# B and C of a Mamba block, four channel blocks side by side in the TensorE array, with a new set of task times

## The chip, the cores and the metric

The kernel runs on one core of one Trainium2 chip. The metric is the device time of one execution in microseconds (us). A core has a matrix engine (TensorE, PE in the profile, with its weight loads as PEld), a vector engine (VectorE, DVE), an activation engine (ScalarE, ACT), a general engine (GpSimd, POOL) and a queue engine that starts transfers here (SyncE, SP). Each engine works through its own list of instructions in order and waits on semaphores for the others.

## The reference

A block of four residual layers on x of 2 x 2048 tokens and 512 channels, in float32:

```python
x = x + rwkv(layernorm(x))          # a recurrence over the tokens (wkv)
x = x + ffn(layernorm(x))           # silu(x Wg) * (x Wu), times Wd; 1376 wide, weights looked up in a table of 16
x = x + mamba(layernorm(x))
x = x + ffn(layernorm(x))           # same weights

def mamba(s):                       # 1024 channels, 16 states per channel, rank 128
    x, gate = s @ in_proj           # then x: causal convolution of 4 taps, + bias, silu
    u = silu(conv(x) + b)
    ssm = u @ x_proj.T              # 160 columns: 128 of dt_lr, 16 of B, 16 of C
    delta = softplus(dt_lr @ dt_proj.T + dt_b)
    # for every token: h = h * exp(delta * A) + (delta * u) * B ;  y = sum over the states of h * C
    return ((y + u * D) * silu(gate)) @ out_proj.T
```

The change concerns `ssm`, and within it the 32 columns of B and C.

## The kernel before

The kernel has two stages. The first computes the RWKV layer in chunks of 512 tokens, the looked-up weights, and the first feed-forward of the first 256 tokens. It ends near 700 us. The second stage is the subject: 16 chunks of 256 tokens (TB), each with a first feed-forward (`f1`), the front of the Mamba layer (`front`), its scan over the tokens (`scan`), the output projection (`project`) and a second feed-forward (`f2`). A 2048-token sequence is eight chunks, and the state is carried from chunk to chunk.

**Order of the work.** Nothing is scheduled automatically. `Line.at(t, fn)` enters a task with a time; at the end all tasks are sorted by their times and emitted in that order, so the times in the dictionary `AT` fix the order of every engine's list. The unit is a slot: one chunk's scan has 32 slots (SLOTS), one for each pair of channel block and quarter of the states. While chunk w is scanned, the same 32 slots also hold the projection and second feed-forward of chunk w-1, the front of chunk w+1, and the first feed-forward of chunk w+2. `step_size` of a chunk is cut into two halves of four channel blocks, each of two quarters q: the first half is computed in the window before (`step0`), the second in the chunk's own window (`step1`; `step1a` in the first chunk). Weights are loaded in pieces of 256 KB through a ring of 18 buffers by `Stream`, some 8 slots ahead (LEAD).

**The scan.** Per channel block c4 and quarter q of the states: `grow` (L852) multiplies delta*u by B for four states on POOL and adds the carried state (L855); `decay` (L862) computes exp(delta*A) on ACT into PSUM, two states at a time, with three buffers; `run` does the recurrence (L872), the product with C (L873) and keeps the last state (L875) on DVE; `fold` adds the states on POOL (L882, L887, L888). In the last chunk PE adds them instead (`spread`, L896). `load` fetches B and C, spread over the partitions, from DRAM (bcd) with transfers of 512 KB (bc). After a channel pair, DVE closes y (L918, L919).

**The other tasks** named below: a layernorm has its statistics on DVE (L601, L602: mv), its root on POOL (L603 to L606: rs, nrs), its scaling on ACT (L612, L613: nm, xn), a transposition on PE (L618) and a copy on ACT (L619: xnT). A feed-forward has gate and up products (L659: pg, gu), a silu on ACT (L677, L680: hT), a product on DVE (L686, L689) and the down product (L639: po), whose sum DVE adds to x (L643). The front has its products (L712), three taps on DVE (L732) and silu on ACT (L738: u). `step_size` has products with dt_proj (L776), activations (L780 to L786), a logarithm (L790: lt), corrections on DVE (L793, L794), the close on POOL (L799, L800), and the carried state's factor (L807 on ACT, L814 on POOL). The silu of the gate is L848 (sg). Exp, log and silu need different tables in ACT, so that ACT_TABLE_LOAD stands between them.

**The task that is changed**, `x_product`, multiplies u by x_proj: for each of two column groups (128 columns of dt_lr, then 32 of B and C) eight products, one per channel block, are added in PSUM (L752). Then ACT copies B and C (bcs, L755) and dt_lr (dtl, L757), and SP stores bcs to DRAM (L759). All of this is one task at slot `x`.

Of the kernel before, what the change touches and what calls it, by code (L numbers as in the profile page):

```python
# [8 lines left out]
F32 = mybir.dt.float32  # L9
I32 = mybir.dt.int32  # L10
AF = mybir.ActivationFunctionType
ALU = mybir.AluOpType
# [3 lines left out]
P = 128  # L16
# [8 lines left out]
ND = DI // P  # L25
NS = 16
RK = 128
# [3 lines left out]
TB = 256  # L31
# [29 lines left out]
def block_kernel(ctx: ExitStack, tc: tile.TileContext, a: dict, out: bass.AP):  # L61
    nc = tc.nc
    V, S, G, PE = nc.vector, nc.scalar, nc.gpsimd, nc.tensor
# [4 lines left out]
    ident = const.tile([P, P], F32, name="ident")  # L68
# [14 lines left out]
    with ExitStack() as pa:  # L83
        wpool = pa.enter_context(tc.tile_pool(name="a_w", bufs=1))
# [4 lines left out]
        wk = pa.enter_context(tc.tile_pool(name="a_wk", bufs=11))  # L89
# [28 lines left out]
        for k in range(4):  # L118
# [7 lines left out]
                  y=0.413, x=-3.46, stats=-3.029, stat=0.083, each=0.062, copy=0.119, fmul=0.867,  # L126
                  opened=-3.355, mean=-2.71, scale=-2.177, turn=-2.106, out=3.964, outs=0.02,
                  add=0.188, bits=(-3.02, 29.13), marks=(-4.09, 10.75), ahead=0.503, ff=(11.44,
                  31.66), ffln=10.705, fgate=0.559, fdown=2.36, times=0.284)
        NBITS = 8  # L130
        line = Line()
# [361 lines left out]
    with ExitStack() as pb:  # L493
        NWS, LEAD = 18, 8.0
        wpool = pb.enter_context(tc.tile_pool(name="b_w", bufs=1))
# [10 lines left out]
        wk = pb.enter_context(tc.tile_pool(name="b_wk", bufs=2))  # L506
# [10 lines left out]
        for tl, nm in ((cw, "conv_w"), (cb, "conv_b"), (dtb, "dt_b"), (dcol, "D"), (acol, "A_log")):  # L517
# [7 lines left out]
        wxp = wpool.tile([P, ND, RK + 2 * NS], F32, name="wxp")  # L525
        wdt = wpool.tile([P, DI], F32, name="wdt")
        nc.sync.dma_start(wxp, a["x_proj"].rearrange("(k p) d -> p k d", p=P))
        nc.sync.dma_start(wdt, a["dt_proj"])

        nchunk = NTOK // TB  # L530
        NJ = TB // P


        AT = dict(total=0.13, y=1.08, decay=1.1, grow=1.5, fold=2.75, gates=(2.59, 0.82, 24.96,
                  26.99), front=(6.05, 6.48, 7.41, 8.16), f2=(8.75, 8.93, 12.67, 14.17, 14.38,
                  16.88), f1=(21.88, 21.98, 24.35, 24.27, 29.8, 25.63), f2d=16.39, f1d=30.14,
                  x=11.42, step0=20.87, step1=9.48, step=2.56, exp=0.62, log=1.16, fix=2.12,
                  du=3.52, carry=3.52, zero=4.38, proj=2.49, frontln=3.04, f2ln=5.92, f1ln=18.95,
                  store=29.71, taps=1.03, conv=0.04, unit=1.86, add=0.6, silu=-0.29, hT=0.36,
                  scale=0.19, turn=0.82, g1ln=-5.01, g1=0.94, g1s=1.17, late=7.66, step1a=-5.72,  # L540
                  ahead=12.53, spread=2.01, gsilu=0.64)
        line = Line()
        xs = {}

        def mm(name="ps"):
            return mmp.tile([P, 2, TB], F32, tag="mm", name=name)
# [45 lines left out]
        def ln(t, ci, box):  # L592
# [29 lines left out]
            for j in range(NJ):  # L622
                line.at(t + AT["scale"] + 0.1 * j, scale, j)
                line.at(t + AT["turn"] + 0.1 * j, turn, j)

        def residual(times, ci, lhsT, src):

            po, n = [], len(times)
            w = [stream.piece(t, t + 0.01, src(i)) for i, t in enumerate(times)]

            def first():
                for j in range(NJ):
                    po.append(mmp.tile([P, C], F32, tag="mm", name="po"))

            def one(i):
                lw = lhsT(i)
                m = lw.shape[0]
                for j in range(NJ):
                    PE.matmul(po[j], lhsT=lw[:, j * P : (j + 1) * P], rhs=w[i]["w"][:m],  # L639
                              start=(i == 0), stop=(i == n - 1))  # L640

            def add(j):
                V.tensor_tensor(xs[ci][j], xs[ci][j], po[j], ALU.add)  # L643

            line.at(times[0], first)
            for i, t in enumerate(times):
                line.at(t + 0.005, one, i)
            for j in range(NJ):
                line.at(times[-1] + 0.3 + AT["add"] + 0.15 * j, add, j)

        def feed_forward(t_ln, times, td, dtd, ci):
# [39 lines left out]
            for i, ti in zip(range(0, NF, 2), times):  # L691
                d = 0.65 if i + 1 < NF else 0.3
                for j in range(2):
# [3 lines left out]
                    line.at(tj + 0.005, half, i, j, w)  # L697
                line.at(ti + d + AT["silu"], gate, i)
                line.at(ti + 2 * d + AT["hT"], close, i)
            residual([td + dtd * i for i in range(NF)], ci, lambda i: hT[i], lambda i: wff[i][:, 2 * C :])  # L700

        def front(t_ln, times, tx, ci, box):

            ln(t_ln, ci, box)
            xin, ps = {}, {}

            def product(cp, w):
                ps[cp] = mm()
                for j in range(2):
                    wj = w[j]["w"].rearrange("p (k f) -> p k f", k=KC)  # L710
                    for k in range(KC):
                        PE.matmul(ps[cp][:, j, :], lhsT=wj[:, k, :], rhs=box["xnT"][:, k, :],  # L712
                                  start=(k == 0), stop=(k == KC - 1))

            def copy(cp):
                two = slice(2 * cp, 2 * cp + 2)
                x = xin[cp] = wk.tile([P, 2, TB + KCONV - 1], F32, tag="xin", name="xin")
                if ci % (SEQ // TB) == 0:
                    G.memset(x[:, :, : KCONV - 1], 0.0)
                else:  # L720
                    S.copy(x[:, :, : KCONV - 1], cst[:, two, :])
                S.copy(x[:, :, KCONV - 1 :], ps[cp])
                S.copy(cst[:, two, :], x[:, :, TB:])
                for j in range(2):
                    c = 2 * cp + j
                    S.activation(ps[cp][:, j, :], ps[cp][:, j, :], AF.Identity,  # L726
                                 bias=cb[:, c : c + 1], scale=cw[:, c, KCONV - 1 : KCONV])

            def taps(cp, j):
                c = 2 * cp + j  # L730
                for i in range(KCONV - 1):
                    V.scalar_tensor_tensor(ps[cp][:, j, :], xin[cp][:, j, i : i + TB],  # L732
                                           cw[:, c, i : i + 1], ps[cp][:, j, :], ALU.mult, ALU.add)

            def unit(cp):
                if cp == 0:
                    box["u"] = up.tile([P, ND, TB], F32, tag="u", name="u")
                S.activation(box["u"][:, 2 * cp : 2 * cp + 2, :], ps[cp], AF.Silu)  # L738

            for cp, tp_ in enumerate(times):  # L740
                w = [stream.piece(tp_, tp_ + 0.01, a["in_proj"][2 * cp + j]) for j in range(2)]
                line.at(tp_ + 0.005, product, cp, w)
                line.at(tp_ + AT["conv"], copy, cp)
                for j in range(2):
                    line.at(tp_ + AT["taps"] + 0.35 * j, taps, cp, j)
                line.at(tp_ + AT["unit"], unit, cp)

            def x_product():
                p2 = mm()
                for j, (lo, m) in enumerate(((0, RK), (RK, 2 * NS))):  # L750
                    for c in range(ND):
                        PE.matmul(p2[:m, j, :], lhsT=wxp[:, c, lo : lo + m], rhs=box["u"][:, c, :],  # L752
                                  start=(c == 0), stop=(c == ND - 1))
                bcs = wk.tile([2 * NS, TB], F32, tag="bcs", name="bcs", bufs=1)
                S.copy(bcs, p2[: 2 * NS, 1, :])  # L755
                box["dtl"] = wk.tile([P, TB], F32, tag="dtl", name="dtl")
                S.copy(box["dtl"], p2[:, 0, :])  # L757
                box["bcd"] = bcd_p.tile([2 * NS, TB], F32, tag="bcd", name="bcd")
                nc.sync.dma_start(box["bcd"], bcs)  # L759

            line.at(tx, x_product)

        def step_size(t, box, half):

# [185 lines left out]
        for w in range(-1, nchunk + 1):  # L950
# [14 lines left out]
            if -1 <= w < nchunk - 1:  # L965
                boxes[w + 1] = {}
                late = AT["late"] if w == 0 else 0.0
# [69 lines left out]
```

## Time and profile before

| | |
|---|---|
| three runs | 3670.57 us median (3670.43 to 3672.81) |
| profiled execution, its own time | 3668.55 us |
| its span, first to last instruction | 3666.7 us |
| granted TensorE clock, mean | 0.973 |
| instructions | 43341 |
| start of the scan of the first chunk | 789.8 us |
| last scan instruction starts | 3584.3 us |
| grows of one chunk (POOL, L852) | 32 of 2.36 us |
| scans of one chunk (DVE, L872) | 64 of 1.22 us |
| x_product's matrix instructions (L752) | 512, in 16 chunks |

How to read the lines that follow. The totals of the page name an engine, its busy time, its share of the span and its instructions. A line of the windows names a stretch, its length, then the busy time of PE, PEld, DVE, ACT and POOL with the number of instructions, then the clock, the share of DMA and GB/s. A line of waits names who waited (engine, tile, line) and for whom, the total in us, the number of times, and the longest. A line of the timeline has start and length in us, engine, line, operation, output<-input, shapes, and in brackets the idle time ahead of it with its releaser. A float32 product is two passes of the array, and the profile counts each pass, so that "x16" is eight products.

### The profile page before, as it was taken

Reading aid. Unit: us, or ns where it says so; the run is one execution under the profiler, and the core shown is the slowest. Engines: PE = TensorE matmul, PEld = TensorE weight load, DVE = VectorE, ACT = ScalarE, POOL = GpSimd, SP = SyncE. Lnnn points to the kernel's source line nnn. Section 1 sums busy time; section 2 is a strip of 40 time slices with the busy share of each in tenths; the row PEclk is TensorE's granted clock in tenths of the full one; section 3 lists DMA queues with packets and bytes.
Section 4 is the critical chain, followed back from the end, with each engine's and each line's share of the span. In section 5 each row is a group of like instructions: output and inputs, shape, how many; then the busy total and the mean of one; then the engine's idle time right before and its main releaser. Section 6 shows DMA issues by size and latency. Waiting matters only on the chain. (4 is left out here: it accounts for less than half of the span.)

```text
span 3666.7 us, 43341 instructions
## 1 busy us (share of the span) xinstructions
PE 3389.0 (92%) x12577; PEld 2292.7 (63%) x12592; DVE 3215.8 (88%) x4880; ACT 2744.4 (75%) x4870; POOL 3015.4 (82%) x2801
## 2 busy tenths in 40 slices
PE   7898999777999999999999999999999999998698
PEld 3443444365676767676767666676767676766475
DVE  7999999459898989999999999999989898989882
ACT  5566776487787878787888878787878787878661
POOL 2555666358999999999999999999999999999850
PEclk9999999898999999999999999999999999999799
DMA  2121111244656565565656565656565555554441
GB/s 112 41 72 66 58 66 66 89 164 139 192 185 190 183 189 184 179 203 166 216 169 206 168 213 167 209 177 200 176 204 179 190 184 190 187 187 136 137 147 60
DMA packets 266876, 572.49 MB, mean 156 GB/s; under 512 B 29840, under 2 KB 31504, under 8 KB 266640
## 3 DMA queue, kind: packets, MB, share of 16 engines
q1 hardware_dynamic: 266640, 569.73, 47.9%
q8 instruction: 101, 1.65, 0.2%
q14 instruction: 135, 1.11, 0.1%
HBM read 543.14 MB, written 26.48 MB: 155 GB/s over the span
## 5 line engine op out<-in xcount | busy, mean ns | idle before, releaser
L872 DVE TENSOR_TENSOR_SCAN h<-h,db 128x512 f32<-128x512 f32 x1024 | 1252.2, 1223 | 124.1 <-ACT h L862 100.1
L852 POOL TENSOR_TENSOR db<-du,bc 128x1024 f32<-128x1024 f32 x512 | 1206.3, 2356 | 37.1 <-PE y L896 35.5
L862 ACT ACTIVATE h<-dl,acol 128x256 f32<-128x256 f32 x2048 | 955.4, 475 | 302.7 <-DVE hst L875 265.1
L873 DVE TENSOR_TENSOR db<-h,bc 128x512 f32<-128x512 f32 x1024 | 708.0, 691 | 35.9
L882 POOL TENSOR_TENSOR db<-db 128x512 f32<-128x512 f32 x480 | 609.4, 1270 | 0.0
L639 PE MATMUL po<-w,hT 128*128 128x512 f32 x1364 | 600.6, 592 | 0.0
L659 PE MATMUL pg<-xnT,w 128*128 128x256 f32 x2480 | 555.2, 381 | 1.8 <-ACT xnT L619 1.8
L659 PE MATMUL gu<-xnT,w 128*128 128x256 f32 x2480 | 555.7, 379 | 0.0
L659 PEld LDWEIGHTS pg<-xnT,w 128*128 128x128 f32 x2480 | 472.9, 191 | 69.6 <-ACT xnT L619 6.4
L659 PEld LDWEIGHTS gu<-xnT,w 128*128 128x128 f32 x2480 | 472.3, 190 | 69.0 <-issue 6.7
L639 PEld LDWEIGHTS po<-w,hT 128*128 128x128 f32 x1364 | 259.7, 190 | 286.9 <-issue 271.8
L888 POOL TENSOR_TENSOR acc<-db 128x256 f32<-128x256 f32 x480 | 348.4, 726 | 37.7
L376 PE MATMUL ps<-xnT,wrvk 128*128 128x512 f32 x768 | 347.4, 604 | 11.7 <-DVE e L401 9.9
L862 ACT ACT_TABLE_LOAD x206 | 264.3, 1283 | 3.6
L376 PEld LDWEIGHTS ps<-xnT,wrvk 128*128 128x128 f32 x768 | 148.7, 195 | 183.9 <-issue 162.3
L842 PE MATMUL ps<-xnT,w 128*128 128x256 f32 x1024 | 235.6, 384 | 26.6 <-DMA w<-in_in_proj 13.5
L842 PEld LDWEIGHTS ps<-xnT,w 128*128 128x128 f32 x1024 | 196.3, 193 | 70.9 <-DVE x L643 23.0
L712 PE MATMUL ps<-xnT,w 128*128 128x256 f32 x1024 | 236.1, 391 | 1.4 <-ACT xnT L619 1.4
L639 PE MATMUL po<-w,u 128*128 128x512 f32 x512 | 231.8, 601 | 2.1 <-DVE u L919 2.1
L712 PEld LDWEIGHTS ps<-xnT,w 128*128 128x128 f32 x1024 | 200.8, 198 | 36.4 <-ACT h L862 3.3
L437 POOL TENSOR_TENSOR d<-aa,opq 128x512 f32<-128x512 f32 x32 | 58.2, 1818 | 195.7 <-DVE opq L422 183.5
L732 DVE SCALAR_TENSOR_TENSOR ps<-xin,cw,ps 128x256 f32<-128x256 f32 x384 | 187.1, 488 | 26.0 <-ACT ps L726 15.5
(155 smaller groups left out, 5059.9 us busy)
## 6 DMA issues: line engine op xcount, KB each, us to landing
w<-wff SPq DMA_DIRECT2D x1023, 256.0 KB, 2.7
bc<-bcd SPq DMA_DIRECT2D x256, 512.0 KB, 4.2
w<-in_in_proj SPq DMA_DIRECT2D x256, 256.0 KB, 2.7
w<-in_out_proj SPq DMA_DIRECT2D x128, 256.0 KB, 2.7
wff<-t SPq DMA_DIRECT2D x11, 768.0 KB, 3.9
w<-wff SPq DMA_DIRECT2D x11, 768.0 KB, 4.3
x<-in_x SPq DMA_DIRECT2D x8, 1024.0 KB, 5.2
x1d<-x SPq DMA_DIRECT2D x8, 1024.0 KB, 4.3
```

What stands on the lines that cost most here:

```text
L376: PE.matmul(ps, lhsT=wrvk[:, k, lo : lo + P], rhs=chunk["xnT"][:, k, :], start=(k == 0), stop=(k == KC - 1))
L639: PE.matmul(po[j], lhsT=lw[:, j * P : (j + 1) * P], rhs=w[i]["w"][:m], start=(i == 0), stop=(i == n - 1))
L659: PE.matmul(to[:m], lhsT=w[:, k, :m], rhs=box["xnT"][:, k, :], start=(k == 0), stop=(k == KC - 1))
L712: PE.matmul(ps[cp][:, j, :], lhsT=wj[:, k, :], rhs=box["xnT"][:, k, :], start=(k == 0), stop=(k == KC - 1))
L732: V.scalar_tensor_tensor(ps[cp][:, j, :], xin[cp][:, j, i : i + TB], cw[:, c, i : i + 1], ps[cp][:, j, :], ALU.mult, ALU.add)
L842: PE.matmul(ps[:, j, :], lhsT=wj[:, k, :], rhs=box["xnT"][:, k, :], start=(k == 0), stop=(k == KC - 1))
L852: G.tensor_tensor(d, box["du", half][:, c4, :].unsqueeze(1).to_broadcast([P, 4, TB]), bs[half, q], ALU.mult)
L862: S.activation(h[:, n, :], box["dl", half][:, c4, :], AF.Exp, scale=acol[:, 4 * half + c4, col : col + 1])
L872: V.tensor_tensor_scan(flat(h), flat(h), flat(d[:, two, :]), 0.0, ALU.mult, ALU.add)
L873: V.tensor_tensor(d[:, two, :], h, cs[half, q][:, two, :], ALU.mult)
L882: G.tensor_tensor(d[:, 0:2, :], d[:, 0:2, :], d[:, 2:4, :], ALU.add)
L888: G.tensor_tensor(to, d[:, 0, :], d[:, 1, :], ALU.add)
```

## The change

In `x_product` the 128 columns of dt_lr are computed as before. The 32 columns of B and C use a quarter of the array's columns. Now the eight channel blocks go by turns into four column groups (`tile_position`), so that four partial sums of two blocks each stand in four groups of 32 partitions of PSUM. ACT copies all 128 partitions to `bc4`, and one product with four identities stacked on each other (`group`, 128 x 32) adds the four groups. The task becomes four: the products at `x`, the two copies at `x + xtake`, the added product at `x + xsum`, the copy bcs and its store at `x + xstore`. The stacked identities are made by three additions on DVE at the start of the stage.

All times in `AT` are set anew. Among them: x 11.42 to 10.48, step1a -5.72 to -3.33, g1ln -5.01 to -1.38 and g1 0.94 to 1.74 (layernorm and start of the feed-forward of chunk 1 in the first chunk's window), y 1.08 to 1.66, total 0.13 to -0.92, du 3.52 to 3.19, store 29.71 to 26.27, ahead 12.53 to 14.3.

```diff
+        group = wpool.tile([P, 2 * NS], F32, name="group")
+        V.tensor_tensor(group, ident[:, : 2 * NS], ident[:, 2 * NS : 4 * NS], ALU.add)
+        for i in (2, 3):
+            V.tensor_tensor(group, group, ident[:, i * 2 * NS : (i + 1) * 2 * NS], ALU.add)
...
-        AT = dict(total=0.13, y=1.08, decay=1.1, grow=1.5, fold=2.75, gates=(2.59, 0.82, 24.96,
-                  26.99), front=(6.05, 6.48, 7.41, 8.16), f2=(8.75, 8.93, 12.67, 14.17, 14.38,
-                  16.88), f1=(21.88, 21.98, 24.35, 24.27, 29.8, 25.63), f2d=16.39, f1d=30.14,
-                  x=11.42, step0=20.87, step1=9.48, step=2.56, exp=0.62, log=1.16, fix=2.12,
-                  du=3.52, carry=3.52, zero=4.38, proj=2.49, frontln=3.04, f2ln=5.92, f1ln=18.95,
-                  store=29.71, taps=1.03, conv=0.04, unit=1.86, add=0.6, silu=-0.29, hT=0.36,
-                  scale=0.19, turn=0.82, g1ln=-5.01, g1=0.94, g1s=1.17, late=7.66, step1a=-5.72,
-                  ahead=12.53, spread=2.01, gsilu=0.64)
+        AT = dict(total=-0.92, y=1.66, decay=1.09, grow=1.71, fold=2.53, gates=(2.32, -0.06, 25.2,
+                  27.22), front=(6.05, 6.48, 7.41, 8.09), f2=(8.63, 8.83, 12.65, 14.15, 14.31,
+                  16.86), f1=(21.85, 21.96, 25.19, 24.31, 30.18, 25.64), f2d=16.42, f1d=29.87,
+                  x=10.48, step0=20.92, step1=9.46, step=2.3, exp=0.92, log=1.24, fix=2.22, du=3.19,
+                  carry=3.26, zero=4.36, proj=2.66, frontln=3.05, f2ln=5.98, f1ln=18.62,
+                  store=26.27, taps=1.07, conv=0.11, unit=1.91, add=0.55, silu=-0.27, hT=0.46,
+                  scale=0.39, turn=1.33, g1ln=-1.38, g1=1.74, g1s=1.12, late=7.96, step1a=-3.33,
+                  ahead=14.3, spread=2.9, gsilu=0.73, xtake=0.12, xsum=0.8, xstore=1.59)
...
             def x_product():
-                p2 = mm()
-                for j, (lo, m) in enumerate(((0, RK), (RK, 2 * NS))):
-                    for c in range(ND):
-                        PE.matmul(p2[:m, j, :], lhsT=wxp[:, c, lo : lo + m], rhs=box["u"][:, c, :],
-                                  start=(c == 0), stop=(c == ND - 1))
+                p2 = box["p2"] = mm()
+                for c in range(ND):
+                    PE.matmul(p2[:, 0, :], lhsT=wxp[:, c, :RK], rhs=box["u"][:, c, :],
+                              start=(c == 0), stop=(c == ND - 1))
+                for c in range(ND):
+                    g = slice(c % 4 * 2 * NS, (c % 4 + 1) * 2 * NS)
+                    PE.matmul(p2[g, 1, :], lhsT=wxp[:, c, RK:], rhs=box["u"][:, c, :],
+                              start=(c < 4), stop=(c >= ND - 4), tile_position=(0, c % 4 * 2 * NS))
+
+            def x_take():
+                box["bc4"] = wk.tile([P, TB], F32, tag="bc4", name="bc4", bufs=1)
+                S.copy(box["bc4"], box["p2"][:, 1, :])
+                box["dtl"] = wk.tile([P, TB], F32, tag="dtl", name="dtl")
+                S.copy(box["dtl"], box["p2"][:, 0, :])
+
+            def x_sum():
+                PE.matmul(box["p2"][: 2 * NS, 1, :], lhsT=group, rhs=box["bc4"], start=True, stop=True)
+
+            def x_store():
                 bcs = wk.tile([2 * NS, TB], F32, tag="bcs", name="bcs", bufs=1)
-                S.copy(bcs, p2[: 2 * NS, 1, :])
-                box["dtl"] = wk.tile([P, TB], F32, tag="dtl", name="dtl")
-                S.copy(box["dtl"], p2[:, 0, :])
+                S.copy(bcs, box["p2"][: 2 * NS, 1, :])
                 box["bcd"] = bcd_p.tile([2 * NS, TB], F32, tag="bcd", name="bcd")
                 nc.sync.dma_start(box["bcd"], bcs)
 
             line.at(tx, x_product)
+            line.at(tx + AT["xtake"], x_take)
+            line.at(tx + AT["xsum"], x_sum)
+            line.at(tx + AT["xstore"], x_store)
```

## The prediction

> **What bounds the kernel now.** I read the page's engine totals first, and distrust them here:
>
> ```profile
> PE 3389.0 (92%) x12577; PEld 2292.7 (63%) x12592; DVE 3215.8 (88%) x4880; ACT 2744.4 (75%) x4870; POOL 3015.4 (82%) x2801
> ```
>
> TensorE (PE) looks like the limit. But the totals mix an RWKV stage (to about 700 us), 16 Mamba chunks and a tail. So next the windows of one chunk, and the waits of POOL over twelve chunks (1094 to 3182 us):
>
> ```profile
> 2860.00:3036.00 176.00, 171.67 (x673) 123.35 (x672) 161.22 (x267) 143.90 (x263) 168.53 (x170) 0.99 0.58 189
> POOL rs L603 <- DVE mv L602: 3.7, 7, 0.9
> POOL dl L799 <- DVE lt L794: 2.5, 1, 2.5
> POOL h L814 <- ACT h L807: 1.6, 4, 0.8
> POOL xin L719 <- DVE ps L732: 1.4, 1, 1.4
> ```
>
> The first line gives PE, weight loads, DVE, ACT and POOL busy in 176 us: 171.7, 123.4, 161.2, 143.9, 168.5. The other four are all that POOL waits for in 2088 us: 9.2 us, under 0.8 per chunk. Its other 7 us per chunk are gaps of some 78 ns before instructions that need POOL's own last result (L888, L855, L887). POOL runs without a pause: **POOL sets the period**, 176.4 us between two closes at L799 where nothing waits (2971.36 to 3147.76). PE is idle 4 to 5 us per chunk, and none of that reaches POOL.
>
> DVE is just behind. The same window's waits of DVE, then three timeline lines:
>
> ```profile
> DVE h L872 <- ACT h L862: 74.2, 58, 3.5
> DVE h L872 <- POOL db L855: 14.7, 10, 1.5
> ...
> 2925.05 1.23 DVE L872 TENSOR_TENSOR_SCAN h<-h,db 128x512 f32<-128x512 f32 x1 [3.46 <-ACT h L862]
> 2970.60 0.69 DVE L794 TENSOR_TENSOR lt<-lt,ps 128x512 f32<-128x512 f32 x1
> 2971.36 1.27 POOL L799 TENSOR_TENSOR dl<-dl,lt 128x512 f32<-128x512 f32 x1
> ```
>
> Once per chunk (third scan) DVE waits some 1.5 us for POOL. After that ACT makes it lose time (74.2/12 = 6.2 us per chunk, 3.46 of it at the tenth scan), so that by scan 24 lt ends at 2971.29 and POOL takes it 0.07 later. POOL and DVE are level there; behind it DVE gains ground again.
>
> The first Mamba chunk is different:
>
> ```profile
> POOL rs L603 <- DVE mv L602: 13.0, 2, 9.1
> POOL dl L799 <- DVE lt L794: 4.8, 1, 4.8
> POOL h L814 <- ACT h L807: 4.0, 1, 4.0
> ...
> 785.68 3.62 PE L659 MATMUL pg<-xnT,w 128*128 128x256 f32 x16
> 824.94 1.97 PE L659 MATMUL ps<-xnT,w 128*96 128x256 f32 x8 [2.84 <-ACT hT L680]
> 844.98 0.69 DVE L643 TENSOR_TENSOR x<-x,po 128x512 f32<-128x512 f32 x1 [2.10 <-PE po L639]
> 890.48 0.68 DVE L601 BATCH_NORM_STATS2 st<-x 128x6 f32<-128x512 f32 x1
> ```
>
> From 778 to 895 POOL waits 21.8 us: on the step size at the start, then at two layernorms. The first needs the feed-forward of chunk 1, which PE runs from 785.68 to about 845.5; the second (892.2) needs DVE, busy nearly throughout since 848.
>
> **What the Trainium skill says.** "Perfetto Trace Analysis", section "Identifying the Most-Contended Engine", takes the engine of highest occupancy as the bottleneck, and for TensorE points to LDWEIGHTS busy instead of matmul busy. The trace agrees on the second: PE's 92% is not the bound, its weight loads are at 63%. "TensorE: Matmul & The Clock Gate", section "Packing small matmuls", gives 2.38 times for three column tiles of 32. No run here shows it yet. "TensorEngine Tiling (Array Packing)", "Key Properties": a change of tiling mode drains TensorE; not shown here either. "ScalarE: Activation LUTs", "What ACT_TABLE_LOAD costs": 1283 ns, plus a drain of 1380. The trace agrees on the first (264.3 us over 206 loads = 1283); the drain does not show, since the activation after a load starts some 10 ns after its end.
>
> **The products.** A product of 256 columns is two passes; sixteen passes start 3.45 us apart in the timeline (2862.89 to 2866.34), so 0.216 each. B and C now take 16 passes = 3.45 us per chunk. Four column groups side by side: four rounds, 0.86 us, if all overlap; the skill's ratio (0.79 per tile) makes an estimate of 1.1; 3.45 if nothing does. I take 1.1. The product with the stacked identities adds two passes, 0.43. It stands directly behind in PE's queue, and must wait for ACT's new copy (0.35, priced by dtl L757, plus queueing): 0.5 to 1.1 us in which all of PE stands. Net for PE: -1.9 + 0.5 to 1.1, about -1 us per chunk; +1.5 at worst, with a drain more. Below the 4 to 5 us that PE idles both vanish: **zero on the path**. The three additions that build the stacked identity are DVE work at the start of the stage, where DVE idles 7 us before 720. Zero.
>
> **ACT.** Per chunk: one more copy (0.35) and, by the two kernels' instruction lists, 33 table loads for 31 (2 x 1.283 = 2.57), 2.9 us. ACT is busy 143.9 of 176, so the sum fits; the place matters. The two copies of x_take now stand ahead of lt (L790): 0.7 us, and up to 1.2 more if PE's four groups don't overlap. L794 starts 1.87 us after lt is ready (2968.73 to 2970.60), which covers it. Scans 25 to 26 can stall 0.5 to 1.7. In return a decay moves ahead of the layernorm's nm (L612), where ACT waited 5.54 us at 2920.55: DVE has a scan of 1.93 us to run in its stall of 3.46, and a table load leaves that stretch too. I expect some 3 us less stall before lt.
>
> **POOL.** Same instructions, two swaps per chunk: the closes L799/L800 of two quarters go up past a grow (2.6 us) and past a fold (2.0). Their slack before was about 4 and 9.4 us: zero. The quarter that is level at 2971 keeps its place, and its lt should come about 2 us earlier.
>
> **SP.** The store of bcd goes behind a pair of bc loads; out_x and bc pairs change places with weight loads that stand some 8 slots (44 us) ahead of use. POOL never waited for a DMA in these chunks: zero. In the first chunk the load of x for chunk 1 falls behind the first bc pair and four weight loads; its normalization comes later anyhow.
>
> **Steady chunks.** What can be won is POOL's own wait: 9.2 us, and 0.3 behind it. The lt waits and the memset (3.9) should go, the layernorms half. I take -5; bounds -9.5 and 0. Between 895 and 1094 POOL waits 2.0 more, same causes: -2 (bounds -2, 0).
>
> **First chunk.** The second half's step size is moved back (step1a), so the first decays come before it: first scan some 9 us earlier, first grow too. POOL then stops at the second half's close and at the layernorm all the same. The normalization for chunk 1 moves behind ACT work: adding up ACT's rows, PE starts that feed-forward at about 789.4 instead of 785.7. PE's stop of 2.84 at the end shrinks to 0.7, so it ends 1.4 later. DVE has then run one scan more (1.93), and the taps start about 1 later. Sum at 892: +0.5, call it 0; the start of x_product's copies moves by -2.4 to +0.2 and with it the whole: bounds -3 and +3.
>
> **Tail.** Chunk 15 is PE-bound from 3464 to 3525. One group of y products (1.73) moves behind the feed-forward, while xnT comes 2.1 later behind two decays: -1 (bounds -2, +1).
>
> **Sum.** 0 - 2 - 5 - 1 = -8 on the profiled execution's 3668.55 (span 3666.7 and 1.85 around it): 3660.5. The median, 3670.57, is 2.0 above that execution: **3662.5 us**.
>
> **Rivals.** (1) Nothing moves: the first chunk is 3 late, layernorm waits stay: 3668 to 3673. For it: POOL is at its own pace and the change takes nothing from it. (2) Slower: DVE overtakes POOL as the bound. ACT's two added table loads stand near scans 53 to 56, where decays lead scans by only 0.1 to 2.3 us. If the 2.9 us reach DVE, its reserve (1.5 at scan 3) is used up; it decides once DVE's stalls grow by over 1.6 us per chunk. Price (2.9 - 1.6) x 14 = 18 us, with x_take's waiting 35: 3689 to 3706. Against: the stall at scan 10 shrinks. (3) PE is the bound after all: 1.9 x 16 = 30 us: 3640. Against: POOL's waits. (4) The column groups don't overlap: PE does 1.5 us more per chunk out of 4 to 5 idle, and lt may lose its lead: 3663 to 3668.
>
> **Numbers.** Forecast 0.42, rival 1 0.30, rival 2 0.18, rival 3 0.07, rival 4 0.03. A measurement of this kernel tells 0.2%, 7.3 us, from no change; the forecast lies just beyond it, and about a third of its own spread (3655 to 3668) falls inside. Faster 0.46, within 0.34, slower 0.20. The range 3648 to 3686 takes in the bounds, rival 1 and the near part of rival 2; rival 3 and the far part stay out.
>
> **What would show it.** Right: POOL's waits from 1094 to 3182 near 4 us, period 176.4, the DVE stall at scan 10 under 1.5, PE's busy time down with no effect. Wrong: POOL waiting over 1 us per chunk for lt or mv; a period under 175.5, which would make PE the bound; a second layernorm in the first chunk away from 892 by over 3 us.

## The result, and the profile after

The changed kernel takes 3681.72 us (median of 8 runs, 3679.4 to 3686.51), the kernel before 3671.12 beside it (8 runs, 3666.61 to 3672.81). The ratio is 1.003, with a 95% interval of 1.0019 to 1.0041: slower by 10.6 us, where 8 less were forecast. The profiled execution took 3682.14 us, with a span of 3680.4.

Lines after the change lie 6 further down in the layernorm, feed-forward and front and 23 further down from `step_size` on (L872 is L895 now). New are L759 (dt products), L763 (B and C), L768 and L770 (the copies bc4 and dtl), L773 (group product). The page's totals:

```profile
PE 3374.3 (92%) x12624; PEld 2291.7 (62%) x12624; DVE 3218.2 (87%) x4883; ACT 2780.2 (76%) x4911; POOL 3018.8 (82%) x2801
```

TensorE has 14.7 us less to do and ACT 35.8 more; POOL's and DVE's work is the same. The windows of one chunk after (176 us, with the same columns as before):

```profile
2874.00:3050.00 176.00, 168.40 (x671) 122.04 (x670) 160.68 (x265) 145.89 (x264) 168.13 (x170) 0.99 0.60 187
```

PE works 168.4 of 176 us instead of 171.7. The waits between 1094 and 3182 us:

```profile
DVE h L895 <- ACT h L885: 74.1, 69, 2.4
PE tr L624 <- ACT xn L619: 61.6, 42, 3.3
DVE hT L695 <- PE ps L665: 30.3, 11, 4.1
PE ps L773 <- ACT dtl L770: 14.8, 12, 1.2
DVE h L895 <- POOL db L878: 13.1, 9, 1.5
POOL rs L609 <- DVE mv L608: 7.9, 11, 2.3
...
POOL dl L822 <- DVE lt L817: 5.0, 4, 3.1
POOL h L837 <- ACT h L830: 5.0, 20, 0.8
```

POOL waits 17.9 us for other engines instead of 9.2: 4.2 more ahead of the layernorms' root (L609), 3.4 more ahead of the carried state's product (L837), 2.5 more ahead of the closes (L822), and 1.4 less for the taps. Over twelve chunks (48 closes) POOL takes 2127.19 us instead of 2116.99: 10.2 more, 8.7 of them in these waits. DVE's wait for ACT has not shrunk (74.1), and PE's wait for xn has grown from 40.4 to 61.6.

Where that stands in a chunk shows in PE's timeline, first before, then after. Each starts 29 to 30 us behind its chunk's third scan (2900.84 and 2914.67), the scan at which DVE waits for POOL in both kernels:

```profile
2930.04 7.07 PE L712 MATMUL ps<-xnT,w 128*128 128x256 f32 x32
2937.00 0.66 PE L618 MATMUL tr<-ident,xn 128*128 128x128 f32 x4
2938.03 0.66 PE L618 MATMUL tr<-ident,xn 128*128 128x128 f32 x4 [0.38 <-ACT xn L613]
2938.52 7.07 PE L712 MATMUL ps<-xnT,w 128*128 128x256 f32 x32
```

```profile
2944.66 2.97 PE L718 MATMUL ps<-xnT,w 128*128 128x256 f32 x13
2950.90 0.66 PE L624 MATMUL tr<-ident,xn 128*128 128x128 f32 x4 [3.28 <-ACT xn L619]
2952.84 1.11 PE L624 MATMUL tr<-ident,xn 128*128 128x128 f32 x4 [1.28 <-ACT xn L619]
2953.75 8.03 PE L718 MATMUL ps<-xnT,w 128*128 128x256 f32 x32
...
2979.84 1.07 PE L763 MATMUL ps<-u,wxp 128*32 128x256 f32 x16
2982.15 0.62 PE L773 MATMUL ps<-bc,group 128*32 128x256 f32 x2 [1.24 <-ACT dtl L770]
```

Two things are to be seen. PE now reaches the second layernorm's transpositions early and stops, 3.28 us, then 1.28 more for the second xn. (In seven of nine chunks the kernel before has a stop of 1.5 us there, and another of 1.5 us ahead of the layernorm before it, which is gone now.) And the 32 passes behind that take 8.03 us instead of 7.07: the first passes start 0.427 us apart, the later ones 0.216. The granted clock of the first 4.1 us behind the transpositions, in the windows after and then before (last columns: clock, DMA share, GB/s):

```profile
2953.70:2957.80 4.10, 4.10 (x17) 3.46 (x16) 3.89 (x9) 3.71 (x9) 3.94 (x5) 0.76 0.05 9
```

```profile
2938.50:2942.60 4.10, 4.10 (x21) 3.65 (x20) 3.89 (x10) 4.00 (x11) 3.94 (x4) 1.00 0.35 114
```

Why the second xn is late shows on ACT:

```profile
2949.70 0.30 ACT L618 ACTIVATE nm<-mv,nrs 128x1 f32<-128x1 f32 x1 [3.67 <-POOL nrs L612]
2950.03 0.81 ACT L619 ACTIVATE xn<-x,nm,rs 128x512 f32<-128x512 f32 x1
2950.75 0.97 ACT L885 ACTIVATE h<-dl,acol 128x256 f32<-128x256 f32 x2
2951.66 0.28 ACT L618 ACTIVATE nm<-mv,nrs 128x1 f32<-128x1 f32 x1
2951.97 0.81 ACT L619 ACTIVATE xn<-x,nm,rs 128x512 f32<-128x512 f32 x1
```

ACT waits for POOL's nrs, and a pair of decays stands between the two xn; before, both xn came ahead of it.

The first chunk. Its lines that answer to those shown before:

```profile
789.99 6.21 PE L665 MATMUL pg<-xnT,w 128*128 128x256 f32 x16 [5.02 <-ACT xnT L625]
796.03 3.62 PE L665 MATMUL gu<-xnT,w 128*128 128x256 f32 x16
...
829.47 1.97 PE L665 MATMUL ps<-xnT,w 128*96 128x256 f32 x8 [0.47 <-ACT hT L686]
```

```profile
852.75 0.23 POOL L609 TENSOR_SCALAR rs<-mv 128x2 f32<-128x2 f32 x1 [8.96 <-DVE mv L608]
896.18 0.22 POOL L609 TENSOR_SCALAR rs<-mv 128x2 f32<-128x2 f32 x1 [8.47 <-DVE mv L608]
```

The feed-forward of chunk 1 starts at 789.99, and its first 16 passes take 6.04 us from start to start instead of 3.45. The second layernorm comes 3.9 us later (896.18 for 892.26).

The start of a chunk's scan, after minus before: +4.5 in the second chunk, +5.6, +5.9, +7.0 in the next, then up to +15.7 in the last. The last scan is 14.8 later, the span's end 13.7. Besides the start, one step stands out: +9.4 to +12.5 in the chunk at the border of the two sequences, 3 us in one chunk.

### The profile page after: what moved, and what is told of

It is laid out like the page before. It is cut to its first block, busy times and chain, and to the rows that moved or that the text cites. A ratio compares the mean times of both kernels' runs of the same rounds, so it can differ in the third digit from the quotient of the medians.

```text
span 3680.4 us, 43474 instructions
## 1 busy us (share of the span) xinstructions
PE 3374.3 (92%) x12624; PEld 2291.7 (62%) x12624; DVE 3218.2 (87%) x4883; ACT 2780.2 (76%) x4911; POOL 3018.8 (82%) x2801
## 5 line engine op out<-in xcount | busy, mean ns | idle before, releaser
L895 DVE TENSOR_TENSOR_SCAN h<-h,db 128x512 f32<-128x512 f32 x1024 | 1252.3, 1223 | 122.8 <-ACT h L885 96.5
L865 PE MATMUL ps<-xnT,w 128*128 128x256 f32 x1024 | 237.2, 386 | 17.2 <-ACT sg L871 8.3
L718 PE MATMUL ps<-xnT,w 128*128 128x256 f32 x1024 | 249.5, 406 | 2.3 <-ACT xnT L625 2.3
L718 PEld LDWEIGHTS ps<-xnT,w 128*128 128x128 f32 x1024 | 211.5, 208 | 41.4 <-issue 6.7
L865 PEld LDWEIGHTS ps<-xnT,w 128*128 128x128 f32 x1024 | 196.8, 193 | 61.7 <-issue 15.7
```

What stands on the lines that cost most here:

```text
L865: PE.matmul(ps[:, j, :], lhsT=wj[:, k, :], rhs=box["xnT"][:, k, :], start=(k == 0), stop=(k == KC - 1))
L895: V.tensor_tensor_scan(flat(h), flat(h), flat(d[:, two, :]), 0.0, ALU.mult, ALU.add)
```

## The experiments

**Theory**, from the two traces: the new task times make PE stop at the second layernorm, its clock falls to half, scans 24 and 25 come late, and POOL waits; the start costs some 4 us besides. (Scans are counted within a chunk.) **Rivals**: the two copies ahead of lt; PE's stop at the group product; the products themselves. Each kernel ran beside the kernel before on the same chip; the kernel before took 3670.39 to 3672.63 us there, so medians of different runs can differ by 2 us for that reason alone. The table gives, from the single instructions of each trace, means over the nine chunks 3 to 7 and 11 to 14 (those not next to the border of the two sequences): the period between third scans, PE's stop before the transpositions, the number of passes of the front's products behind it that start over 0.3 us apart (slow passes), and the starts of the last front pass and of scan 25, counted from the third scan.

| kernel | ratio to before, 95% | period | stop | slow passes | last front pass | scan 25 |
|---|---|---|---|---|---|---|
| before | | 176.74 | 1.2 | 0 to 8, mean 1.8 | +44.77 | +70.40 |
| after | 1.0019 to 1.0041 | 177.65 | 3.3 | 5 to 10, mean 6.7 | +47.12 | +72.17 |
| e1 products alone | 1.0207 to 1.0234 | 182.77 | 1.6 | 0 to 8, mean 3.3 | +45.20 | +70.47 |
| e2 times alone | 1.0113 to 1.0141 | 180.57 | 3.3 | 5 to 12 | +47.92 | +75.01 |
| e3 start undone | 1.0015 to 1.0028 | 177.44 | 3.3 | 5 to 7 | +46.91 | +71.94 |
| e4 take behind lt | 1.0064 to 1.0089 | 179.21 | 3.3 | 4 to 11 | +47.41 | +71.87 |
| e5 xn before decay | 0.9985 to 1.0001 | 177.06 | 3.3 | 2 to 10 | +46.42 | +71.50 |
| e6 PE kept warm | 0.9990 to 1.0006 | 176.65 | 0 | 0 | +45.72 | +70.80 |
| e7 both and start | 0.9992 to 1.0008 | 176.71 | 0 | 0 | +45.72 | +70.82 |
| e8 copies left out | 1.0011 to 1.0024 | 177.44 | 3.3 | 6 to 10 | +47.46 | +71.93 |
| e9 xn and 12 warm | 1.0000 to 1.0016 | 177.29 | 0.6 | 2 | +44.74 | +70.81 |
| e10 start warm too | 0.9995 to 1.0012 | 177.29 | 0.6 | 2 | +44.75 | +70.81 |
| e11 before, less work | 1.0000 to 1.0016 | 177.43 | 3.3 | 6 to 10 | +46.38 | +70.85 |
| e12 x load earlier | 1.0009 to 1.0022 | 177.42 | 0 | 0 | +42.96 | +67.99 |

**e1, products alone.**

```diff
...
-                  x=10.48, step0=20.92, step1=9.46, step=2.3, exp=0.92, log=1.24, fix=2.22, du=3.19,
+                  x=11.42, step0=20.87, step1=9.48, step=2.56, exp=0.62, log=1.16, fix=2.12,
...
+                  ahead=12.53, spread=2.01, gsilu=0.64, xtake=0.12, xsum=0.8, xstore=1.59)
```

> The new products, copies and stacked identities (x_take, x_sum, x_store) with the kernel before's task times. Theory A (the new task times put ACT's work in an order that makes scans 24 and 25 late, and the start dearer; the products themselves cost nothing): POOL's period stays 176.3 to 176.6, its waits for lt, mv and h from 1094 to 3182 us stay under 12 us, total 3668 to 3675. Theory B (the products cost it: PE stands at the group product, or the switch of tiling): the loss stays, period 177.0 to 177.4, total 3679 to 3685.

3752.28 us, ratio 1.022 (1.0207 to 1.0234): both theories missed, and by far. The waits from 1094 to 3182 us, and PE's stop in one chunk:

```profile
PE ps L773 <- ACT dtl L770: 62.1, 11, 5.9
...
POOL rs L609 <- DVE mv L608: 52.8, 12, 7.4
```

```profile
2855.09 1.06 PE L773 MATMUL ps<-bc,group 128*32 128x256 f32 x2 [5.93 <-ACT dtl L770]
2856.08 6.17 PE L665 MATMUL pg<-xnT,w 128*128 128x256 f32 x16
```

With the old times the copies stand behind lt and its decays; PE stands 5.9 us for them and runs the passes behind it at half clock (16 in 6.17 us). POOL then waits 52.8 us for layernorms. That the stop reaches POOL through the feed-forward behind it is my reading; no run tests it. PE's stop at the second layernorm stays short here (1.6 us).

**e2, times alone.**

```diff
...
-                  x=11.42, step0=20.87, step1=9.48, step=2.56, exp=0.62, log=1.16, fix=2.12,
+                  x=10.48, step0=20.92, step1=9.46, step=2.3, exp=0.92, log=1.24, fix=2.22, du=3.19,
...
```

> The old products (B and C as 32 columns, copies behind them in the same task) with the new task times. Theory A: the loss is here; period 177.0 to 177.4, POOL's waits 15 to 20 us over the twelve chunks, the first product of the feed-forward of chunk 1 later by some 4 us, total 3678 to 3684. Theory B: 3667 to 3673.

3717.36 us, ratio 1.0127: worse than either bound. The waits of POOL and ACT:

```profile
POOL dl L799 <- DVE lt L794: 31.9, 11, 4.5
ACT bcs L755 <- PE ps L752: 22.0, 11, 2.0
```

The old products are 2.4 us longer than the packed ones. With the early copies, ACT stands 2.0 us per chunk for them, ahead of lt. PE's stop of 3.3 us and the half clock behind it are here too, with the old products: they come with the times. So products and times don't add: alone they cost 81 and 46 us, together 10.6. What either is worth depends on the other.

**e3, start undone.**

```diff
-                  scale=0.39, turn=1.33, g1ln=-1.38, g1=1.74, g1s=1.12, late=7.96, step1a=-3.33,
+                  scale=0.39, turn=1.33, g1ln=-5.01, g1=0.94, g1s=1.17, late=7.66, step1a=-5.72,
```

> The changed kernel with the five times that rule the first chunk (g1ln, g1, g1s, late, step1a) set back. Theory A: the start's 4 us go, the later chunks keep their 0.85 us each: scans of the second chunk at +0 to +1.5 against the kernel before, period 177.1 to 177.4, total 3676 to 3680. Rival: the start is late through the products in it (PE stands at its group product, ACT has the extra copy), whatever these times: 3680 to 3685.

3679.43 us. The third chunk starts at +1.7 against the kernel before instead of +5.6, and the period stays. But the second chunk still starts at +2.9, and the medians differ by only 2.3, with overlapping intervals: the start is a small part of the loss, and what remains of it is not explained.

**e4, take behind lt.**

```diff
-            line.at(tx + AT["xtake"], x_take)
-            line.at(tx + AT["xsum"], x_sum)
-            line.at(tx + AT["xstore"], x_store)
+            line.at(tx + AT["xtake"] + 0.83 * (ci > 1), x_take)
+            line.at(tx + AT["xsum"] + 1.64 * (ci > 1), x_sum)
+            line.at(tx + AT["xstore"] + 1.35 * (ci > 1), x_store)
```

> The changed kernel with the two copies of x_take behind lt and the four decays after it from the third chunk on, as the kernel before has its copies; the group product goes behind the next feed-forward product, so that PE doesn't stand for the later copies. Theory A1 (the two copies, 0.7 us, ahead of lt make scans 24 and 25 late): the stall before scan 24 falls from 2.4 to about 1.7 us, lt comes 0.7 earlier, POOL's waits fall from 17.9 to 9 to 14 us, period 176.6 to 176.9, total 3674 to 3679. Theory A2 (all of it comes from the earlier layernorm whose second xn stands behind a decay; the copies are covered by the 1.9 us that lt waits for DVE): 3680 to 3684, period 177.1 to 177.4.

3700.83 us: a miss for both. The stall before scan 24 did not move (2.43 us for 2.44), so the copies don't cause it. The kernel made a loss of its own. The store of bcd comes some 10 us later in SP's queue (91 instead of 81 us behind the chunk's first scan). As I read it, the loads of x behind it come late for that reason, and the layernorm with them (DVE waits 16.6 us for x over the twelve chunks, 3.3 in the changed kernel):

```profile
3034.08 0.69 DVE L607 BATCH_NORM_STATS2 st<-x 128x6 f32<-128x512 f32 x1 [0.92 <-DMA x<-x1d]
```

**e8, copies left out**, asks the same question without that side effect.

```diff
-                box["bc4"] = wk.tile([P, TB], F32, tag="bc4", name="bc4", bufs=1)
-                S.copy(box["bc4"], box["p2"][:, 1, :])
+                if ci > 1:
+                    box["bc4"] = const
...
-                S.copy(box["dtl"], box["p2"][:, 0, :])
+                if ci < 2:
+                    S.copy(box["dtl"], box["p2"][:, 0, :])
```

> The changed kernel with x_take's two copies (0.73 us of ACT ahead of lt) left out from the third chunk on: the group product and the step size read a constant tile instead, so the values are not those of the reference, and PE doesn't wait 1.2 us for the copies. Theory A (those copies make lt and the 25th scan late): lt 0.7 us earlier, period 176.4 to 176.7, total 3670 to 3676. Theories B and C (the delay is there before the copies come): lt moves by under 0.2 us, period 177.0 to 177.3, total 3677 to 3682.

3679.53 us. Without the copies and PE's wait for them, the stall before scan 24 is the same 2.44 us; the one before scan 25 falls from 1.46 to 0.89. The copies cost about 0.6 us at scan 25, and 2 to 4 us of the 10.6 in all (2.2 by the medians, 3.7 against the kernel before beside each), with PE's stop at the group product included. Both rivals fall as the main cause.

**e5, xn before decay.**

```diff
-                line.at(t + AT["scale"] + 0.1 * j, scale, j)
+                line.at(t + sc + 0.1 * j, scale, j)     # sc = 0.30 for f2's layernorm, AT["scale"] = 0.39 elsewhere
```

> The changed kernel with one thing set back: in the second layernorm of a window both xn come before the sixteenth pair of decays, as in the kernel before. Theory B (the late second xn makes PE stop twice, 3.3 and 1.3 us, and so the front products, the taps and scans 16 to 24 late): the stop of 1.3 us goes, the front products start some 1.2 us earlier, the stall before scan 24 falls from 2.4 to about 1.3 us, period 176.6 to 176.9 instead of 177.3, total 3673 to 3678. Rival (the copies ahead of lt, or the group product): 3680 to 3684.

3670.64 us, ratio 0.9993: with a pair of decays moved behind one nm and xn on ACT, 11 us are back by the medians. PE, with the stop as before but without the second one:

```profile
2937.69 2.15 PE L624 MATMUL tr<-ident,xn 128*128 128x128 f32 x8 [3.26 <-ACT xn L619]
2939.63 9.05 PE L718 MATMUL ps<-xnT,w 128*128 128x256 f32 x32
```

In this chunk the slow passes (9) take back what the earlier start gave, and its period is 177.6. In the two chunks of the nine with 2 to 6 of them the period is 176.6, in the seven with 8 to 10 it is 177.2 in the mean. The half clock thus looks like a cost of its own; e6 tests that. The nine chunks account for about half of what e5 gains (0.6 us each); it also takes 2.5 us off the chunk at the border and 1.7 off the second, against the changed kernel, and why is open.

**e6, PE kept warm.**

```diff
+                for k in range(heat * (1 - j)):          # heat = 24 in f2's layernorm
+                    PE.matmul(tr[:, k % KC, :], lhsT=ident, rhs=ident, start=True, stop=True)
                 for k in range(KC):
                     PE.transpose(tr[:, k, :], box["xn", j][:, k * P : (k + 1) * P], ident)
```

> The changed kernel with 24 products of 128 columns (identity by identity, into the tile that the transposes then overwrite) ahead of the first transposes of that layernorm, so that PE works through most of its stop of 3.3 us. It is 2.6 us of work more per chunk and no wait less. Theory C (the stop puts TensorE at half clock, 0.427 instead of 0.216 us per product for the next four to eleven products): the slow products behind the transposes go, the front products end 1 us earlier, period 176.6 to 176.9, total 3674 to 3679. If the half clock reaches nothing that POOL waits for: 3680 to 3685. If PE has no room: over 3690.

3672.49 us: PE has 5.5 us more to do per chunk, and the kernel is 9 us faster than the changed one by the medians, level with the kernel before. PE, and the clock behind the transpositions:

```profile
2939.03 5.52 PE L624 MATMUL tr<-ident 128*128 128x128 f32 x48
2944.39 1.04 PE L626 MATMUL tr<-ident,xn 128*128 128x128 f32 x8
2945.26 7.07 PE L720 MATMUL ps<-xnT,w 128*128 128x256 f32 x32
```

```profile
2945.20:2949.30 4.10, 4.10 (x22) 3.63 (x20) 3.89 (x9) 4.00 (x10) 3.94 (x5) 1.00 0.24 69
```

The 24 products are two passes each, 5.5 us and not the 2.6 of the expectation. The front starts no earlier than in the changed kernel, but ends 1.4 us earlier, and scan 25 with it. On PE, nothing but the clock of these passes has changed from there on. The step at the border stays (+2.4 to +6.5 against the kernel before), so the half clock doesn't explain that part.

**e7, both and the start.** e5, e6 and e3 in one.

> The two edits before (xn ahead of the decays, 24 products in PE's stop) and the five times of the first chunk set back, in one kernel. If theories B and C add up and the start is as in the kernel before: period 176.2 to 176.6, total 3664 to 3673, level with or faster than the kernel before. If B and C are the same 1 us told twice: 3671 to 3676. If the copies are the cause: 3677 to 3680.

3672.21 us: level with e6 and e5. The 5.5 us of products hide the earlier xn, so the edits don't add up.

**e9, 12 products.** As e5 and e6, with heat = 12.

> The changed kernel with xn ahead of the decays and 12 instead of 24 identity products (2.6 to 2.8 us in the stop of 3.3), so that they no longer hold the transposes up. If theory C holds in its full form (no product at half clock, front products start 38.2 us after the third scan and end at 44.9 instead of 46.7 to 47.9): scan 25 at +70.0 to +70.5, period 176.2 to 176.5, total 3666 to 3670. If 12 products are too little work to keep the clock up: 4 to 10 slow products, total 3669 to 3673.

3673.61 us. The front ends 1 us earlier than in e6, but scan 25 stays at +70.81: what holds it there is no longer PE. And DVE now waits 12.6 us in all for the loads of x (3.3 in the changed kernel), POOL 11.3 for the layernorms' statistics.

The trace also has half clock at another place. PE's stop ahead of the group product is 1.84 us here (1.24 in the changed kernel), and behind it six of the nine chunks lose clock and three don't. Windows of 3 us in two neighbouring chunks, the fifth and the sixth:

```profile
1560.31:1563.31 3.00, 3.00 (x12) 2.47 (x11) 1.43 (x3) 2.92 (x5) 2.92 (x4) 0.72 0.53 175
1738.74:1741.74 3.00, 3.00 (x15) 2.65 (x14) 1.43 (x3) 2.92 (x5) 2.92 (x4) 1.00 0.53 175
```

The period is 178.44 in the fifth and 176.51 in the sixth; 177.65 in the mean of the six, 176.57 in the mean of the three. e10 has the same stop and again six chunks against three: 177.60 and 176.69. So e9's missing gain stands where this half clock stands. This compares chunks of one execution; no edit tests it.

**e10, start warm too.**

```diff
+                    for k in range(first * (i + j == 0)):   # first = 20 in chunk 1's feed-forward
+                        PE.matmul(ps[0, 0][:, k % 2, :P], lhsT=ident, rhs=ident, start=True, stop=True)
```

> The same, and 20 identity products ahead of the first product of chunk 1's feed-forward, where PE stands 5.0 us. If the half clock there is the larger part of the start's 4 us: that product takes 3.45 instead of 6.0 us, the feed-forward ends some 2.5 earlier, the chunks after it start 1 to 2.5 us earlier, total 3664 to 3668. If DVE or POOL is late there for another reason: as the kernel before this one, within 1 us.

3672.01 us, ratio 1.0004: no difference from e9 that can be told. The products were themselves at half clock and too many:

```profile
785.80 6.16 PE L675 MATMUL pg<-ident 128*128 128x128 f32 x40
791.79 3.62 PE L667 MATMUL pg<-xnT,w 128*128 128x256 f32 x16
```

The feed-forward's first product ends where it did in e9 (795.25 for 795.15), so the run doesn't tell what the half clock costs there.

**e11, before with less work**, the opposite test: the kernel before, with PE made to stop.

```diff
-                    for k in range(KC):
+                    n = KC // 2 if cp == 1 and ci > 1 else KC
+                    for k in range(n):
```

> The kernel before, with half of the second front product left out from the third chunk on (8 of its 16 passes for K blocks 2 and 3; the values are not the reference's): TensorE has 1.7 us less to do per chunk, and its stop before the second layernorm's transposes grows from 1.5 to about 3.3 us. Theory C: TensorE falls to half clock there in most chunks (4 to 10 slow products instead of none in most), the front products end 1 to 2 us later and scan 25 comes 0.2 to 1 later; the kernel is not faster for its missing work: 3671 to 3680. Rival (TensorE's work counts, or nothing does): no slow products, 3665 to 3671.

3672.9 us beside 3670.39. PE in one chunk:

```profile
2943.57 0.66 PE L618 MATMUL tr<-ident,xn 128*128 128x128 f32 x4 [3.27 <-ACT xn L613]
2944.60 0.77 PE L618 MATMUL tr<-ident,xn 128*128 128x128 f32 x4 [0.37 <-ACT xn L613]
2945.16 8.69 PE L713 MATMUL ps<-xnT,w 128*128 128x256 f32 x32
```

With 1.7 us less to do per chunk, 24 us in all, the kernel is at best level. The stop is now 3.3 us in every chunk, the slow passes 6 to 10, and POOL's time for the 48 closes grows by 6.7 us. Its wait ahead of the carried state's product is 5.6 us, as in the changed kernel (5.0; 1.6 before). So the long stop, with its half clock, costs POOL time without any new task time. But POOL's waits for the layernorms and the closes hardly grow here (3.9 and 2.5 us, 3.7 and 2.5 before), while in the changed kernel they do (7.9 and 5.0). This run thus reproduces a part of the loss.

**e12, x load earlier.** e9 with the start undone, and:

```diff
-                line.at(t + 18.0, load_x, w + 2)
+                line.at(t + 16.0, load_x, w + 2)
```

> The kernel of 12 identity products and early xn, with the five times of the first chunk set back and the load of the chunk after next's x ahead of seven weight loads on SP's queue (18 to 16 slots). If its missing gain was that load (DVE waits 12.6 us for it over twelve chunks, POOL 11.3 us for DVE behind it): both fall under 5 us, period 176.2 to 176.5 in nearly every chunk, total 3663 to 3668, faster than both kernels. If only the start's times act: 3669 to 3672.

3677.67 us, a miss. DVE no longer waits for x, and scan 25 comes at +67.99, the earliest of all. But the period is 177.5 in nearly every chunk. So the loads were not what e9 lacked. PE, busy 172.4 of 177.5 us with the 12 products, now stops elsewhere, and its next 32 passes take 9.73 us instead of 7.07. In the second and third chunk, with a period of 176.6, the granted clock is at half there for 3.4 us; in the chunks from the fourth on, for 6.8. That PE sets the period here is my reading, and no run tests it:

```profile
3028.49 9.73 PE L667 MATMUL pg<-xnT,w 128*128 128x256 f32 x32 [3.31 <-ACT h L887]
```

No version is shown to beat the kernel before; e5 is level with it.

## Why the prediction was wrong, step by step

- **POOL sets the period: right for both kernels.** 8.7 of the 10.2 us lost over twelve chunks are POOL's waits.
- **The products: right in size, wrong in "zero on the path".** B and C take 1.07 us (1.1 was taken), the stop at the group product is 1.24 (0.5 to 1.1), and PE's net gain is 0.9 per chunk. The step that failed is "below the 4 to 5 us that PE idles both vanish: zero on the path", and with it "none of that reaches POOL". It counted PE's idle time as a sum and put its place at nothing. The new times gather it in one stop of 3.27 us at the second layernorm (e2 has that stop with the old products; e1, with the new products and the old times, doesn't). That stop has a price: half clock for 5 to 10 passes, each 0.21 us late, 1.0 to 2.1 us on the front. e6 takes the half clock away, and the period falls from 177.65 to 176.65; e11 brings it into the kernel before, and the period rises from 176.74 to 177.43. By which wait the late front reaches POOL is argued and not shown: scan 25 stands at +70.80 in e6 and at +70.81 in e9, whose periods differ by 0.6 us, so its place alone does not set the period. The Trainium skill warns of such stops: "TensorE: Matmul & The Clock Gate", section "HAM oscillation — how this bites in real kernels", speaks of TensorE gaps over about 3.4 us. I had quoted that page for something else. The measurement goes below that: here 3.27 us did it in every chunk, and in the kernel before a stop of 1.5 us at this place was followed by half clock in 4 of the 10 chunks that have it (chunks 3 to 15).
- **"A decay moves ahead of the layernorm's nm ... some 3 us less stall before lt": the first half right, the second wrong.** The stall of 3.46 us at scan 10 is gone. In its place DVE now stalls 2.44 us at scan 24 and 1.46 at scan 25, where it had none, so that its wait for ACT is the same in all. ACT then waits 3.67 us for POOL's nrs at the second layernorm, a point fixed by POOL (35.0 us behind the third scan in both kernels). What DVE had won did not pass it, as I read the two traces. I had looked at the layernorm whose nm moves, and not at the next, where a pair of decays came between the two xn. Undoing that alone gives back 11 us (e5), with most of the half clock still there.
- **x_take's copies covered: nearly right.** They cost 0.6 us at scan 25 (e8).
- **Steady chunks -5: wrong by 15.** Measured +10.2, 3 of it in the chunk at the border. Even with the clock held (e6) POOL's waits are 9.2 us, as before: scan 24 is then 1.1 us earlier than before but scan 25 0.4 later. The gain that was forecast isn't there under these times.
- **First chunk 0, bounds -3 and +3: outside, +4.5.** PE started at 789.99 (789.4 was said), but its first product after the stop took 6.04 for 3.45 us. The feed-forward ended 4.5 later where 1.4 were said; 2.6 of the 3.1 between are this half clock. x_product's first copy came 0.7 earlier (753.64 for 754.33), within the -2.4 to +0.2 that was said.
- **Tail -1:** the delay falls by 2.0 from the last chunk's start to the end. Right.
- **Rival 2** was right in its sign and wrong in its mechanism: DVE's wait for ACT did not grow (74.1 us for 74.2). The two table loads per chunk came (33 for 31), but DVE's stalls at scans 53 to 59, where they were to act, are 0.6 us per chunk instead of 1.2. Its price would have been 18 us or more. That the measured time lies within the range is luck: the range reached so far up for a mechanism that did not act.

Still open: the rest of the start's delay that e3 leaves, the 3 us at the border of the sequences, and what on ACT holds scans 24 and 25 at +65.9 and +70.8 in e6 and e9, where the front's earlier end no longer helps.

## What to carry to other kernels

An engine's idle time is not a store to draw on: look at the length of its longest stop and where it lies. Giving TensorE less work (e11) or letting it run ahead (the new times) here turned stops of 1.5 us into one of 3.3, and the passes behind that one ran at half clock. Read the starts of single passes behind each stop, not the mean clock. When some chunks of one execution have the half clock and others don't, compare their periods: e9 and e10 show the cost without another run. In this kernel, a change that shortens one task and a set of times made for it had to be judged together (81 and 46 us alone, 10.6 together). And the order of a few small instructions on a third engine can be worth as much as the whole change: e5 moved one pair of decays.

## What the runs showed of the hardware that was not expected

- After a stop of 3.3 us the next 2 to 12 passes of 256 columns start 0.427 us apart instead of 0.216, a varying number from chunk to chunk of one execution. Work without a use in the stop (e6) kept the rate at 0.216.
- Shorter stops do it in some chunks only: 1.84 us in six of nine (e9, and again e10), 1.5 us in four of ten (the kernel before). The stops of 1.24 us at the group product did it in none of the nine chunks of the changed kernel.
- Four column groups of 32 do run side by side in float32: 16 passes in 1.07 us, where 16 passes one after the other take 3.45. In the changed kernel's first chunk they start in fours, 0.006 to 0.007 us apart within a four and some 0.2 us from one four to the next. No drain is seen: between the dt products, these and the group product the profile lists no gap but the 1.24 us for ACT.
